# One unbroken line of expert tiles, independent scatters, and ranks by prefix sums, in a fused attention and mixture-of-experts kernel

## The chip, the core and the metric

The kernel runs on one core of a Trainium2 chip. The core has five engines, each with an instruction queue of its own that it works off in order: PE (TensorE, matmul and transpose), DVE (VectorE), ACT (ScalarE), POOL (GpSimd) and SP (SyncE, which issues most of the DMAs). Engines wait for each other, and for DMAs, by semaphores. PE loads the stationary operand of a matmul with a separate instruction, which the profile lists as PEld. The metric is the device time of one execution in microseconds; a profile adds, for one execution, a record of each instruction.

## The reference

Four batches of 1024 rows of 128 numbers pass through four residual stages, each on a normalised copy of the rows. In short form:

```
x = x + attention_a(layernorm(x))   # 8 heads of 128, with a relative-position term
x = x + experts(layernorm(x))       # 8 experts, the best 2 for each row
x = x + attention_b(layernorm(x))   # causal, 16 query heads of 8, one key/value head
x = x + experts(layernorm(x))       # the same weights again

def experts(x):
    scores = softmax(x @ Wg.T)                    # 8 per row
    val, idx = top_k(scores, 2)
    val = val / (val.sum(-1) + 1e-9)
    comb = (one_hot(idx) * val[..., None]).sum(-2)
    out = 0
    for e in range(8):
        a, b = split(x @ W1[e].T + b1[e], 2)      # 256 each
        out += ((a * sigmoid(b)) @ Wo.T + bo) * comb[..., e]
    return out
```

Everything is in float32.

## The kernel before

**Stages.** The program is attention a, experts f, attention b, experts g, in this order; f and g are the two uses of the experts. All of x stays in SBUF. In each stage the order of instructions on every engine is that in which the program's text issues them: the order is written by hand, as Python generators that are advanced in turn, one `yield` being one place where something else may be put between. An engine that meets an instruction whose input isn't there stands still, and so does all that is queued behind it.

**The experts' method.** A row is computed for its two experts only. The 2048 (row, expert) pairs of a batch are sorted by expert, each expert's share is rounded up to whole tiles of 128 rows, and so a batch never needs more than `TILES` = 23 tiles, of which each belongs to one expert. The sorted rows lie in DRAM (`sorted_rows[b]`), and so do the experts' results (`stores`).

**`dispatch` (L203 to L343)** sorts one batch for one of the two stages:

- `norm_steps` (L87): means and variances on DVE, `rstd` as a power on POOL (L101), `shift` on DVE (L103), eight scalings on ACT. Then POOL sets the last column of the copy to 1 (the row sums to zero, so that column is known from the rest, and the experts' weights are prepared so that it carries the bias).
- Two halves of four transposes each, `lnps` (L217), copied to SBUF by ACT; eight small matmuls for the gate, `gp` (L223); softmax and the two best experts on DVE (L247 to L281), with a mask of 128 x 8 tiles x 8 experts for each choice.
- `rank`: how many earlier pairs go to the same expert. `sel` is the sum of the two masks. One matmul with `before` (a strict triangle of ones) counts the earlier rows within a tile (L287), and eight with `ones`, each 8 columns narrower than the last, add the tiles before (L289). A ninth tile of zeros at the end makes the totals.
- From these on DVE the place of each pair (`places`), and the expert of each of the 23 tiles (`experts`, L322 to L330).
- Sixteen scatters (L335), indirect DMAs issued by POOL, each of which writes 128 rows into `sorted_rows[b]`. The framework sees sixteen writes to one tensor.

The parameters `far` and `at_once` say how many yields separate the dispatch's parts, and after how many scatters one comes. The first three dispatches of f run inside attention a, one beside each of its later batches (from L676); the fourth runs beside the first steps of experts f. Those of g run beside attention b once a batch's rows are finished (in `causal_attention`, L1051), and what is left by its end runs in experts g.

**`experts_tiles` (L728)** computes one batch as twelve pairs of tiles with two further steps to drain. A step p does, in this order: a `fetch` (L710) of four tiles of sorted rows from DRAM into one of four slots of `ring`, issued by SP; `first`, one matmul of 512 columns for each of two tiles (`h`, L745), a sigmoid on ACT (L749) and a product on DVE (`u`, L751); `turn_hidden` of the pair before, four transposes (L759) and a copy on ACT (L767); in every second step `turn_rows`, four transposes of the next fetched tiles (L733, the tile is named `xgps`) with a copy on ACT (L735); and `second` of the pair two back (`yp`, L777), whose bias is added on DVE (L784) before SP stores the result (L788). The two drain steps hold no `first`. The next batch's first two fetches are issued in them, and its first `turn_rows` follows at once.

**`combine` (L812)** brings a batch's results back: sixteen gathers by indirect DMA on POOL (L833), and for each the weighted addition to x on DVE (L820). `at_once` sets how many gathers go out in a step, and an addition is issued once 2 * `at_once` further gathers have been. For g the finished rows then leave for the output.

**`ffn` (L850)** runs the batches one after the other, and advances beside each step the generators listed for it: the fourth dispatch, the combines, and two calls of `b_prep` (L878, the queries and keys of attention b for batches 0 and 1). Seen as one list, f has 56 steps:

```
0: [sends("f", B - 1, (2, 2))], 20: [combine("f", 0, 1)], 37: [combine("f", 1, 2)], 39: [b_prep(0)],
48: [combine("f", 2, 2)], 49: [b_prep(1)],
```

In g the dispatches that are left are chained: one ends before the next begins. The last combine of g stands behind all of it, and nothing runs beside it.

Of the kernel before, what the change touches and what calls it, by code (L numbers as in the profile page):

```python
# [18 lines left out]
P = 128  # L19
# [45 lines left out]
def block_kernel(ctx: ExitStack, tc: tile.TileContext, a: dict, out: bass.AP):  # L65
# [21 lines left out]
    def norm_steps(x_b, name, got, xn=None, fine=False):  # L87
# [13 lines left out]
        nc.gpsimd.tensor_tensor(rstd, ve, nhalf, ALU.pow)  # L101
        shift = work.tile([P, NB], F32, tag="ln_sh", name=f"sh_{name}")
# [4 lines left out]
        for t in range(NB):  # L107
            nc.scalar.activation(
                xn[:, t, :], x_b[:, t, :], AF.Identity, bias=shift[:, t : t + 1],
                scale=rstd[:, t : t + 1],  # L110
            )
            if t == 3 or (t % 2 and fine):
                yield
# [44 lines left out]

    earlier = wp.tile([P, E, E], F32, tag="earlier", name="earlier")
# [41 lines left out]
    chosen, sent_off = {}, set()  # L201

    def dispatch(which, b, bank, new_xn, new_xnT, far, at_once):  # L203
# [15 lines left out]
        for _ in range(far):  # L219
            yield  # L220
# [35 lines left out]
        sel = part(NB + 1)  # L256
        dv.memset(sel[:, NB, :], 0.0)
# [16 lines left out]
        dv.tensor_tensor(sel[:, :NB, :], masks[0], masks[1], ALU.add)  # L274
# [11 lines left out]
        flat = sel.rearrange("p t e -> p (t e)")  # L286
        nc.tensor.matmul(rank[:, : (NB + 1) * E], before, flat, start=True, stop=False)  # L287
        for k in range(1, NB + 1):
            nc.tensor.matmul(  # L289
                rank[:, k * E : (NB + 1) * E], ones, flat[:, : (NB + 1 - k) * E],  # L290
                start=False, stop=(k == NB),
            )
# [28 lines left out]
        began = part(TILES)[:1]  # L321
# [10 lines left out]
        yield  # L332
        for t in range(NB):
            for k in range(2):
                nc.gpsimd.indirect_dma_start(  # L335
# [3 lines left out]
                )  # L339
                if t == NB - 1 and k == 1:  # L340
                    sent_off.add((which, b))
# [9 lines left out]
    with ExitStack() as sa:  # L351
# [278 lines left out]
        with tc.manual_schedule():  # L630
            for t in range(-AHEAD, N + 5):
# [44 lines left out]
                if m >= H and m % H < H - 3:  # L676
                    if m % H == 0 and i == 0:
# [4 lines left out]
                            2, 1,  # L682
# [17 lines left out]
    def sends(which, b, pace=(2, 1)):  # L700
        return dispatch(
            which, b, one,
            lambda: fp.tile([P, NB, D], F32, tag="xn", name=f"xn_{which}{b}", bufs=1),
            lambda: fp.tile([P, L], F32, tag="xnT", name=f"xnT_{which}{b}", bufs=1),
# [3 lines left out]
    chunks = (TILES + 3) // 4  # L708
    pairs = (TILES + 1) // 2
    fetched = []  # L710

    def fetch(which, b, c):
        assert (which, b) in sent_off, (which, b)
        n = min(4, TILES - 4 * c)
        xg = ring[:, len(fetched) % 4]
        fetched.append((b, c))
        nc.sync.dma_start(
            out=xg[:, :n, :],
            in_=sorted_rows[b].rearrange("(t p) d -> p t d", p=P)[:, 4 * c : 4 * c + n, :],
        )  # L720
        return xg, n

    def experts_tiles(which, b, stored, come):


        nm = f"{which}{b}"
        experts = chosen[which, b][2]
        turned, hidden, outs = {}, {}, {}  # L728

        def turn_rows(c, xg, n):  # L730
            ps = one(f"xgps_{nm}_{c}")
            for t in range(n):
                nc.tensor.transpose(ps[:, t * P : (t + 1) * P], xg[:, t, :], ident)  # L733
            xgT = fp.tile([P, 4, P], F32, tag="xgT", name=f"xgT_{nm}_{c}", bufs=2)
            nc.scalar.copy(xgT[:, :n, :].rearrange("p t c -> p (t c)"), ps[:, : n * P])  # L735
            turned[c] = xgT

        def first(j):
            at = nc.values_load(
                experts[0:1, j : j + 1], engines=[mybir.EngineType.PE], min_val=0,  # L740
                max_val=(E - 1) * 512,
                skip_runtime_bounds_check_because="one less than a sum of E comparisons, times 512",
            )
            ps = one(f"h_{nm}_{j}")
            nc.tensor.matmul(  # L745
                ps, turned[j // 4][:, j % 4, :], w1[:, bass.ds(at, 512)], start=True, stop=True
            )
            sig = fp.tile([P, HID], F32, tag="sig", name=f"sig_{nm}_{j}", bufs=3)
            nc.scalar.activation(sig, ps[:, HID:], AF.Sigmoid)  # L749
            u = fp.tile([P, HID], F32, tag="u", name=f"u_{nm}_{j}", bufs=4)  # L750
            nc.vector.tensor_tensor(u, ps[:, :HID], sig, ALU.mult)  # L751
            hidden[j] = u

        def turn_hidden(p):
            js = [j for j in (2 * p, 2 * p + 1) if j < TILES]
            ps = one(f"turn_{nm}_{p}")
            for q, j in enumerate(js):
                for k in range(2):
                    nc.tensor.transpose(  # L759
                        ps[:, (2 * q + k) * P : (2 * q + k + 1) * P],  # L760
                        hidden[j][:, k * P : (k + 1) * P], ident,
                    )
                del hidden[j]
            uT = fp.tile([P, 4, P], F32, tag="uT", name=f"uT_{nm}_{p}", bufs=2)
            n = 2 * len(js) * P
            uf = uT.rearrange("p k c -> p (k c)")
            nc.scalar.copy(uf[:, :n], ps[:, :n])  # L767
            return uT, js

        def second(p, uT, js):  # L770
            if p % 2 == 0:
                outs[p // 2] = small(f"yp_{nm}_{p}")
            yp = outs[p // 2]
# [436 lines left out]
```

## Time and profile before

| what | us |
|---|---|
| median of 3 runs (lowest, highest) | 2942.23 (2940.53, 2950.89) |
| the profiled execution, its own time | 2939.64 |
| its span, first to last instruction | 2937.9 |
| mean granted PE clock | 0.952 of full |

| group, in experts g and around it (2654 to the end) | count | busy us | mean ns |
|---|---|---|---|
| h, PE, L745 | 184 | 99.5 | 669 |
| yp, PE, L777 | 368 | 50.8 | 283 |
| turn, PE, L759 | 184 | 29.2 | 280 |
| xgps, PE, L733 | 92 | 15.6 | 294 |
| scatters, POOL, L335 | 32 | 31.0 | 970 |
| gathers, POOL, L833 | 64 | 61.0 | 953 |
| u, DVE, L751 | 92 | 38.0 | 423 |
| uT copies, ACT, L767 | 48 | 27.2 | 568 |

How to read it: a group collects the instructions of one line. PE's float32 matmuls appear as two records each, and records overlap, so that sums of a group's busy time exceed the time it occupies; the distance between the starts of successive groups is what it takes. A row of the timeline gives start, duration, engine, line, operation, output and inputs, shape, count, and in brackets the time the engine had stood idle before it and what ended that. "issue" is a wait that the profile doesn't explain, "remote" a semaphore whose sender it doesn't name.

### The profile page before, as it was taken

What the parts mean: (1) busy time and instruction counts of PE and PEld (TensorE: products, weight loads), DVE (VectorE), ACT (ScalarE), POOL (GpSimd) and SP (SyncE); (2) the same over time, 40 slices, a digit from 0 to 9 for tenths busy, and PEclk for the clock granted to TensorE, in tenths of its full rate; (3) what the DMA queues carried; (4) which work ended last, traced back from release to release, by engine and by line L of the source; (5) the groups of instructions that cost most, each with busy time, mean ns of one, the idle gap of its engine ahead of it and who ended that gap; (6) DMA issues with size and microseconds to landing.
All of it is one profiled execution on the core that took longest, in us unless ns stands there. A gap on an engine that the chain in (4) does not pass through costs nothing. (4 is left out here: it accounts for less than half of the span.)

```text
span 2937.9 us, 46362 instructions
## 1 busy us (share of the span) xinstructions
PE 2768.5 (94%) x18784; PEld 1699.4 (58%) x18784; DVE 1393.6 (47%) x3012; ACT 1334.8 (45%) x2460; POOL 491.1 (17%) x453
## 2 busy tenths in 40 slices
PE   6999999999999999999999887999999999998765
PEld 3465666656665656565656655655465465554543
DVE  2345444454545454545453433556355455662323
ACT  2434344444445344434343343555555655554422
POOL 3121000002000011000010024432121231221154
PEclk9999999999999999999999999899889898999887
DMA  8577566656557565666565123100000000000233
GB/s 212 194 237 238 170 209 191 204 168 213 190 183 221 174 198 190 206 197 210 198 216 169 40 81 86 27 10 1 1 1 1 6 24 1 9 7 25 57 95 91
DMA packets 148485, 363.53 MB, mean 124 GB/s; under 512 B 16160, under 2 KB 71872, under 8 KB 147952
## 3 DMA queue, kind: packets, MB, share of 16 engines
q1 hardware_dynamic: 130128, 316.78, 33.5%
q0 software_dynamic: 15552, 40.97, 5.3%
q10 hardware_dynamic: 2592, 2.82, 0.4%
q8 instruction: 149, 2.44, 0.4%
q14 instruction: 64, 0.52, 0.1%
HBM read 176.69 MB, written 183.76 MB: 123 GB/s over the span
## 5 line engine op out<-in xcount | busy, mean ns | idle before, releaser
L555 DVE CUSTOM_DVE_ANT_0 s<-sp,s 128x1024 f32<-128x1024 f32 x256 | 313.1, 1223 | 392.5 <-PE sp L550 390.7
L550 PE MATMUL sp<-kT,xT 128*128 128x512 f32 x1024 | 484.7, 596 | 3.7 <-ACT kT L509 2.1
L560 ACT ACTIVATE s<-s,nmax 128x1024 f32<-128x1024 f32 x256 | 294.0, 1149 | 416.8 <-DVE nmax L555 416.8
L994 PE MATMUL t_b<-qm,ka_b 32*128 32x512 f32 x1152 | 459.3, 683 | 10.0 <-DVE m L949 8.0
L582 PE MATMUL op<-at,xrep 32*128 32x256 f32 x8192 | 453.0, 377 | 8.6 <-DVE rinv L572 8.6
L582 PEld LDWEIGHTS op<-at,xrep 32*128 32x128 f32 x8192 | 418.6, 186 | 54.5 <-issue 32.9
L942 PE MATMUL s_b<-ka_b,qa_b 32*128 32x128 f32 (+3 forms) x2304 | 439.6, 431 | 2.0 <-DVE xnT_g L248 1.6
L997 ACT ACTIVATE pt_b<-t_b 128x512 f32<-128x512 f32 x576 | 329.3, 611 | 206.3 <-PE t_b L994 163.9
L949 DVE TENSOR_REDUCE m<-s_b 128x1 f32<-128x512 f32 (+3 forms) x480 | 288.9, 650 | 142.9 <-PE s_b L942 119.7
L942 PEld LDWEIGHTS s_b<-ka_b,qa_b 32*128 32x128 f32 x2304 | 275.9, 204 | 74.1 <-issue 21.6
L569 DVE STREAM_TRANSPOSE at<-s 128x1024 f32<-128x1024 f32 x256 | 315.8, 1238 | 0.2 <-ACT s L560 0.2
L522 PE MATMUL rp<-relk,xT 128*128 128x512 f32 x640 | 303.4, 596 | 0.0
L527 ACT COPY xr<-rp 128x1024 f32<-128x1024 f32 x256 | 256.5, 1002 | 84.6 <-issue 52.9
L550 PEld LDWEIGHTS sp<-kT,xT 128*128 128x128 f32 x1024 | 175.0, 191 | 129.4 <-issue 123.3
L994 PEld LDWEIGHTS t_b<-qm,ka_b 32*128 32x128 f32 x1152 | 166.6, 197 | 93.4 <-DVE m L949 50.0
L592 DVE COPY oT<-op 128x256 f32<-128x256 f32 x64 | 24.2, 420 | 401.8 <-PE op L582 401.8
L522 PEld LDWEIGHTS rp<-relk,xT 128*128 128x128 f32 x640 | 116.9, 190 | 131.0 <-issue 129.3
L590 ACT COPY oT<-op 128x256 f32<-128x256 f32 x64 | 20.7, 375 | 355.9 <-PE op L582 355.9
L1015 PE MATMUL o_b<-pt_b,va_b 128*32 128x512 f32 x1152 | 159.6, 678 | 0.0
L335 POOL DMA_INDIRECT sorted<-xn_f,places_f x64 | 62.2, 972 | 466.2 <-DVE places_f L318 311.8
L522 PE MATMUL rp<-w,xT 128*128 128x512 f32 x256 | 121.1, 595 | 0.0
L745 PE MATMUL h_g<-w,xgT_g 128*128 x184 | 99.5, 669 | 14.4 <-ACT xgT_g L735 13.6
(264 smaller groups left out, 3006.1 us busy)
## 6 DMA issues: line engine op xcount, KB each, us to landing
skew<-xr SPq DMA_DIRECT2D x256, 576.0 KB
s<-skew SPq DMA_DIRECT2D x256, 512.0 KB
ring<-sorted SPq DMA_DIRECT2D x40, 256.0 KB
xrep<-stored POOLq DMA_DIRECT2D x16, 512.0 KB
sorted<-ident POOLq DMA_DIRECT2D x4, 1472.0 KB
res_f<-y_f SPq DMA_DIRECT2D x20, 256.0 KB
res_g<-y_g SPq DMA_DIRECT2D x20, 256.0 KB
w<-in_w POOLq DMA_DIRECT2D x16, 256.0 KB
```

What stands on the lines that cost most here:

```text
L522: nc.tensor.matmul(rp[:, c, :], lhsT, rk[:, base + c * 512 : base + (c + 1) * 512], start=True, stop=True)
L527: nc.scalar.copy(xr[:, :L], rp.rearrange("p a c -> p (a c)"))
L550: nc.tensor.matmul(sp[:, c, :], xTs[b][:, i * P : (i + 1) * P], kT[:, c * 512 : (c + 1) * 512], start=True, stop=True,)
L555: nc.vector.tensor_tensor_reduce(out=s, in0=sp.rearrange("p a c -> p (a c)"), in1=s, scale=-1.0, scalar=BIG, op0=ALU.add, op1=ALU.min, acc ...
L560: nc.scalar.activation(s, s, AF.Exp, bias=nmax, scale=-1.0, accum_out=total)
L569: nc.vector.transpose(sums[m][:, i, :], s)
L582: nc.tensor.matmul(ops[g // 2][:, g % 2, :256], xrep[r, j, :], at[r, :, j * 32 : (j + 1) * 32], start=(j == 0), stop=(j == 31),)
L942: nc.tensor.matmul(ps[:, q * w : (q + 1) * w], qa[rows[g], k + q, tok], ka[rows[g], k0 : k0 + w], start=True, stop=True,)
L949: nc.vector.tensor_reduce(m2[:, 4 * g + k : 4 * g + k + nh, c], ps[:, : nh * w].rearrange("p (k c) -> p k c", c=w), AX.X, ALU.max,)
L994: nc.tensor.matmul(ps, ka[rows[g], j * P : (j + 1) * P], qm[rows[g], :], start=True, stop=True)
L997: nc.scalar.activation(pt[:, g, :], ps, AF.Exp, scale=HD ** -0.5)
L1015: nc.tensor.matmul(op[g * 32 : (g + 1) * 32, :], va[:, j, :], pt[:, g, :], start=(j == i), stop=(i == 0 or j == i - 1),)
```

## The change

Four things are changed together.

**One line of experts.** `experts_tiles` no longer runs once a batch. It runs over all 48 steps of the four batches, with three more to drain. In step s: the fetch for step s + 4, then `first` of step s, `turn_hidden` of step s − 2 (s − 1 before), in even steps `turn_rows` for step s + 2, and `second` of step s − 3 (s − 2 before). The turned rows and the hidden values lie in two buffers with four slots each.

```diff
+        rows_T = hold[0].rearrange("p (s t) c -> p s t c", s=4)
+        hidden = hold[1].rearrange("p (s q k) c -> p s q k c", s=4, q=2)
...
+        n = len(steps_of)
+        for s in range(-4, n + 3):
+            if s % 2 == 0 and s // 2 + 2 < len(chunks):
+                fetch(s // 2 + 2)
+            if 0 <= s < n:
+                first(s)
+            if 0 <= s - 2 < n:
+                turn_hidden(s - 2)
+            if s % 2 == 0 and 0 <= s // 2 + 1 < len(chunks):
+                turn_rows(s // 2 + 1)
+            if 0 <= s - 3 < n:
+                second(s - 3)
+            if s >= 0:
+                yield
```

**Scatters.** The sixteen of a batch are declared independent of each other, a memset of one number on POOL stands before each, and each fetch of the batch is made to wait for all sixteen.

```diff
+                nc.gpsimd.memset(between, 0.0)
+                put = nc.gpsimd.indirect_dma_start(
                     out=sorted_rows[b],
...
+                if written_at[which, b]:
+                    tc.declare_no_dep(
+                        put.ins, group=nm, query=mybir.DependencyQuery.ANY_SYNC,
+                        reason="rows at other places",
+                    )
+                tc.add_to_no_dep_group(nm, put.ins)
+                written_at[which, b].append(put.ins)
```

**Ranks.** DVE sums the tiles before each tile by doubling (pairs, fours, eights), with three more additions and a larger memset. PE then does two matmuls of 72 columns, where it did nine.

```diff
-        dv.tensor_tensor(sel[:, :NB, :], masks[0], masks[1], ALU.add)
+        dv.tensor_tensor(sel[:, 1 : NB + 1, :], masks[0], masks[1], ALU.add)
+        dv.tensor_tensor(one_two[:, 2:, :], sel[:, 1 : NB + 1, :], sel[:, :NB, :], ALU.add)
+        dv.tensor_tensor(up_to_four[:, 4:, :], one_two[:, 2:, :], one_two[:, :NB, :], ALU.add)
+        dv.tensor_tensor(
+            sums_before[:, 1:, :], up_to_four[:, 4:, :], up_to_four[:, :NB, :], ALU.add
+        )
...
-        flat = sel.rearrange("p t e -> p (t e)")
-        nc.tensor.matmul(rank[:, : (NB + 1) * E], before, flat, start=True, stop=False)
-        for k in range(1, NB + 1):
+        for k, (w, v) in enumerate(((before, sel[:, 1:, :]), (ones, sums_before))):
             nc.tensor.matmul(
-                rank[:, k * E : (NB + 1) * E], ones, flat[:, : (NB + 1 - k) * E],
-                start=False, stop=(k == NB),
+                rank[:, : (NB + 1) * E], w, v.rearrange("p t e -> p (t e)"),
+                start=(k == 0), stop=(k == 1),
             )
```

**The order around them.** `norm_steps` yields between the power on POOL and `shift`; `dispatch` yields between the halves of `lnps`; scatters in attention a go out two a step. The normalised copies that `sends` uses have two buffers each (one before). `combine` sends two gathers a step and adds six gathers behind; the last one of g sends four a step and adds four behind. The dispatches left over for g run side by side, no longer chained. The lists are:

```diff
-            0: [sends("f", B - 1, (2, 2))], 20: [combine("f", 0, 1)], 37: [combine("f", 1, 2)], 39: [b_prep(0)],
-            48: [combine("f", 2, 2)], 49: [b_prep(1)],
+            0: [sends("f", B - 1, (1, 2))], 22: [combine("f", 0)], 33: [combine("f", 1)],
+            36: [b_prep(0)], 43: [combine("f", 2)], 46: [b_prep(1)],
...
-        rest = itertools.chain(*left, *(sends("g", b, (2, 2)) for b in unsent))
         left = ffn("g", {
-            0: [rest], 21: [combine("g", 0, 1)], 38: [combine("g", 1, 2)], 47: [combine("g", 2, 2)],
+            0: [*left, *(sends("g", b, (1, 2)) for b in unsent)], 22: [combine("g", 0)], 31: [combine("g", 1)], 41: [combine("g", 2)],
         })
```

As the program is built, POOL's queue in g then holds, in this order, `rstd` of batches 2 and 3, the sixteen scatters of batch 2 with the memset of batch 3's copy among them, those of batch 3, and the gathers; before, `rstd` of batch 3 stood behind all scatters of batch 2, and batch 3's scatters alternated with gathers. The second matmul set and the `rank` of batch 2 move into the first steps of experts g, and five of `b_prep(1)`'s fourteen steps stay in experts f, where seven of thirteen did; the rest moves into attention b.

## The prediction

> **What bounds the kernel now.** I read the page's busy shares, then the same shares by stage, then the idle gaps of PE in the two expert stages in the timeline. The stages are attention a (0 to 1650 us), experts f (to 1872), attention b (to 2654), experts g (to the end).
>
> ```profile
> PE 2768.5 (94%) x18784; PEld 1699.4 (58%) x18784; DVE 1393.6 (47%) x3012; ACT 1334.8 (45%) x2460; POOL 491.1 (17%) x453
> ```
> ```profile
> 0.00:1650.00 1650.00, 1602.29 (x11773) 999.53 (x11774) 770.02 (x1626) 700.56 (x1222) 136.40 (x159) 1.00 0.62 196
> 1650.00:1872.00 222.00, 193.09 (x1020) 132.44 (x1021) 87.09 (x258) 100.35 (x216) 77.12 (x76) 0.94 0.26 71
> 1872.00:2654.00 782.00, 770.38 (x4957) 435.17 (x4956) 444.74 (x852) 436.44 (x813) 183.71 (x121) 0.90 0.02 6
> 2654.00:2938.00 284.00, 202.75 (x1042) 132.27 (x1040) 91.73 (x277) 97.41 (x209) 93.84 (x99) 0.84 0.25 69
> ```
>
> Columns of the last four: stretch, its length, busy PE, PEld, DVE, ACT, POOL (instructions), PE's granted clock, DMA share, GB/s. PE is the bound of both attentions: it idles 48 us of 1650 and 12 of 782. In the expert stages it idles 29 of 222 and 81 of 284. What the change can win lies there and in PE work it strikes out.
>
> What an undisturbed expert step costs, from PE's timeline in f:
>
> ```profile
> 1661.85 1.88 PE L745 MATMUL h_f<-w,xgT_f 128*128 x4
> ...
> 1665.33 1.98 PE L745 MATMUL h_f<-w,xgT_f 128*128 x4
> ...
> 1668.48 1.88 PE L745 MATMUL h_f<-w,xgT_f 128*128 x4
> ```
>
> From the first h to the third, two steps (four tiles, one turn_rows) take 6.63 us. So 23 tiles take 38.1 us and four batches **152.5 us**. The stages take more: in f PE runs from 1650.94 to 1861.2 (210.3 us); in g from the first h at 2686.0 to the last yp at 2907.5 (221.5 us). The rest is gaps. Three kinds:
>
> ```profile
> 1743.40 0.63 PE L733 MATMUL xgps_f<-ident,ring 128*128 128x128 f32 x4 [3.15 <-DMA ring<-sorted]
> 1744.71 5.40 PE L745 MATMUL h_f<-w,xgT_f 128*128 x8 [0.67 <-ACT xgT_f L735]
> ```
> ```profile
> 2728.63 0.17 DVE L103 SCALAR_TENSOR_TENSOR sh_g<-mv_g,rstd_g 128x8 f32<-128x8 f32 x1 [18.07 <-POOL rstd_g L101]
> ```
> ```profile
> 2854.18 0.37 ACT L767 COPY uT_g<-turn_g 128x256 f32<-128x256 f32 x1 [9.30 <-remote]
> 2865.43 0.58 ACT L735 COPY xgT_g<-xgps_g 128x512 f32<-128x512 f32 x1 [10.88 <-remote]
> ```
>
> First, a batch boundary: the line drains, the next batch's rows arrive late, then PE's clock is granted at 0.50 for 3.4 us (stretch 1745.3 to 1748.7) and the first h come slowly: 5.40 us for 8 records that take about 3.7 in the steady rows. Second, DVE stands 18 us for a POOL instruction that is queued behind 16 scatters; PE gaps 13.72 us at 2729.3. Third, ACT takes PE's finished results 9 to 11 us late; PE gaps 8.51 and 9.25 us. The last falls in a train of 21 POOL gathers without a pause (2835.7 to 2861.8); a train of 18 in f (1767.9 to 1790.1) has the same in small, PE gaps 2.31, 2.37 and 2.72 us. The trace names no cause.
>
> **Scatters.** They run one at a time, gathers do not:
>
> ```profile
> 2713.42 0.96 POOL L335 DMA_INDIRECT sorted<-xn_g,places_g  x1 [1.54 <-DMA sorted<-xn_g,places_g]
> 2715.92 0.96 POOL L335 DMA_INDIRECT sorted<-xn_g,places_g  x1 [1.55 <-DMA sorted<-xn_g,places_g]
> ...
> 2913.42 0.94 POOL L833 DMA_INDIRECT got_g<-res_g,places_g  x1 [0.30 <-issue]
> 2914.67 0.94 POOL L833 DMA_INDIRECT got_g<-res_g,places_g  x1 [0.30 <-issue]
> ```
>
> Period 2.50 against 1.25 us. Freed, and with the tiny memset before each (an 8-wide one takes 0.11), I take 1.4 to 1.5 us: 16 in 23 us instead of 40. On POOL alone this buys nothing, since PE does not wait for POOL's length; it buys by what is queued behind. The new fetch waits for all 16 of its batch; g3's should end by about step 21 (one step is 3.3 us), and its first fetch is at step 32, so that wait has some 10 steps of cover. If they stayed serial it would still be met, but the g0 gathers behind them would come late (rival C).
>
> **Experts in one line.** Nothing but the batch borders is removed: same transposes, matmuls, copies. Fetch now stands 2 steps (6.6 us) ahead of turn_rows and turn_rows 2 steps ahead of h, where before a boundary started them all at once. Removed in f: boundary gaps 0.86+1.68+0.73, 3.15+0.67+0.73, 2.77+0.67+0.92 = 12.2 us, and the slow restarts, about 1.5 us each, 4.5. In g: 2.60+0.67+0.92 and 3.01+0.68+0.73 = 8.6, 3 for restarts, and the 9.25 gap, counted with the trains. Longer lags (turn_hidden 2, second 3 steps) add a fill and a drain of one step, hidden nowhere but once per stage: 1.5 us.
>
> f, built up: start 2.4 + steps 152.5 + dispatch f3 3.0 (lnps 0.87, gp 1.71, rank 0.43) + b_prep(0) 11.2 = 169, against 210.3: −41. Kept: 3 us of the train's 7.4, since f0's 16 gathers are still free. **f: −37** (0.9 us of lnps_b1 moves to attention b).
>
> g, built up: 152.5 + dispatches 3.5 (g3 3.0, rank_g2 0.43) + the first steps at a half clock, as now, 2.6 + drain 1.5 = 160, against 221.5: −61. The 13.7 us gap goes because rstd_g3 now stands ahead of g2's scatters on POOL, and shift is one yield later on DVE; what is late next is memset xn_g3, behind six of them (9 us), and PE needs that batch only at step 36. The rank_g2 wait (3.16 us, DVE chain) and its work leave the stretch before the first h: −4. Kept of the trains' 18.5: 8. **g: −57.** The tail after the last yp (store, 16 gathers at 1.25, adds, out: 30.4 us) holds the same instructions: 0.
>
> **Combines** start later for f0 (step 22 for 20) and with lag 6, so an add on DVE stands behind its gather less often; before, one waited 5.33 us at 1771.8 and PE gapped 4.40, in g 3.89. f's is inside the −41, g's inside the −61. The price, adds that crowd near attention b, is DVE time beside a busy PE: 0.
>
> **Ranks.** Eighteen records fall to four, eight times:
>
> ```profile
> 1714.54 0.34 PE L287 MATMUL rank_f<-xnT_f,before 128*128 128x72 f32 x2
> 1714.71 1.90 PE L289 MATMUL rank_f<-xnT_f,ones 128*128 128x64 f32 x16
> 1716.47 0.68 PE L745 MATMUL h_f<-w,xgT_f 128*128 x1
> ```
>
> From 1714.54 to 1716.47 is 1.93 us, 0.107 a record whether 72 or 8 columns wide. Four records: 0.43; saved 1.5, eight times **12 us**. The Trainium skill ("TensorE: Matmul & The Clock Gate", Back-to-back issue gap) gives the isolated gap as columns/2.4 + 2.5 ns, and warns that it under-counts small widths. By it the old 360 columns in 9 matmuls, as two records each, are 0.35 us, the new 144 are 0.13: saved 0.2, or 1.8 in all. The row decides: 12. Three more adds on DVE, 72 wide, are some 0.2 us each (estimated from the 0.17 of the 128x8 one above); they lie on the dispatch's own chain, which PE does not wait for in attention.
>
> **Attention a.** A block without dispatch takes 47.09 us; the three with one take 48.33, 52.55, 50.69: +10.3. PE work is 4.5 of it, gaps 0.98 (DVE waits for rstd), 1.74 (second lnps half waits for ACT), 0.69, 0.79. The two yields spread the first two: with ranks −4.2 a dispatch, 12.6 for three. New DVE adds and freed scatters can hurt here: bounds 0 to −12.6 (a loss is rival B), I take **−10**, near the gaps seen.
>
> **Attention b.** Ranks of g0 and g1 −3, b_prep(1)'s late half +2, forced in a burst: **−1**, ±4 as k3, k4 and vp have no row in that place.
>
> Sum: −10 −37 −1 −57 = **−105 us**. Against the profiled execution (2939.64; span 2937.9 plus 1.7 around it) 2834.6; the median of the runs shown is 2.6 higher and their spread 10. Forecast **2834**.
>
> **Rivals.** (B) *Long POOL trains decide.* Free scatters make six new trains of 16 (f0 to f2 in attention a, f3, g2, g3; those of g0 and g1 are broken by affine selects). If each holds back ACT and DVE like the two seen, it costs from 7.4 us (f's) to its whole length, 23, where PE meets it without buffers (g's cost 18.5), and the gather trains keep their full price (+15): 2834 + 15 + 44 to 138 = 2893 to 2987, middle 2940. It decides against the change from 15.2 us a train. For it: two trains of 18 and 21 show it from about the ninth DMA on. Against: each scatter has a memset before it and, past the eighth, a wait for an earlier one's landing; in attention there are more buffers between PE and ACT. Chance 0.15, half of it over 2940.
> (C) *The scatters stay serial* by some other wait. g0's gathers then start at step 29, its adds at 25: DVE waits, some 8 us: 2842. Against: the order of POOL shows no such wait. 0.08.
> (D) *All late starts go*, because lag 6 and the memsets take their cause away: −11 kept, −8 more in attention: 2815. 0.12.
> Main: 0.65.
>
> **How the numbers follow.** The main case runs 2816 to 2855: −12.6 to 0 in attention a, ±4 in b, trains free or at full price (−11 to +15). C and D are within. B is left out, and D's lower part; the ends go a little beyond the main case on both sides for sizes that I mistook: **2806 to 2875**. 0.5% is 14.7 us, about what a measurement here can tell. Below 2925 lie main, C, D and a third of B: 0.90; a third of B is within (0.05), a third slower (0.05).
>
> **What would show it.** Right: from the first h to the last yp 160 us in g, and 169 for PE in f; no ring wait over 1 us at a border; no DVE wait on rstd of 18 us; scatters 1.4 to 1.5 us apart; the three dispatch blocks together 145 to 147; the tail 30 us as before. Wrong: late ACT starts beside scatter trains, attention a longer than 1650, or DVE adds waiting on gathers in g.

## The result and the profile after

| | median us | runs | changed / before |
|---|---|---|---|
| the kernel before | 2947.40 (2937.23 to 2959.76) | 20 | |
| the changed kernel | 2960.31 (2945.73 to 2969.65) | 20 | 1.0038 [1.0021, 1.0054] |

The forecast was 105 us less; the change came out 13 us (0.4%) slower. The profiled execution took 2969.65 us, the slowest of its twenty; its span is 2967.9, the mean granted clock 0.945.

The page's busy shares, and the four stages (columns as before: stretch, length, busy PE, PEld, DVE, ACT, POOL, clock, DMA share, GB/s):

```profile
PE 2760.7 (93%) x18672; PEld 1691.6 (57%) x18672; DVE 1393.6 (47%) x3036; ACT 1333.0 (45%) x2462; POOL 499.6 (17%) x581
```
```profile
0.00:1674.60 1674.60, 1610.98 (x11740) 1003.79 (x11741) 772.75 (x1638) 700.64 (x1222) 140.30 (x207) 0.99 0.59 193
1674.60:1889.10 214.50, 176.89 (x903) 118.80 (x901) 80.96 (x251) 90.84 (x198) 68.77 (x86) 0.90 0.25 72
1889.10:2705.00 815.90, 800.52 (x5178) 453.18 (x5177) 448.82 (x873) 459.61 (x863) 194.81 (x159) 0.91 0.02 7
2705.00:2937.70 232.70, 172.21 (x856) 115.82 (x856) 82.66 (x252) 81.93 (x180) 80.62 (x114) 0.86 0.25 73
```

These borders follow PE's own marks: first xgps_f, last yp_f, first h_g, last yp_g. In the same measure the kernel before took 1651.1, 210.2, 824.8 and 221.6 us. The waits at the batch borders are gone and experts f and g still became longer, 214.5 and 232.7; attention a, too, lost 23 us. PE idles 38 us of experts f and 61 of g.

The DVE timeline in attention a, beside the second train of scatters (1091.9 to 1111.9), shows one such idle time; PE's and POOL's rows of the same time stand below it.

```profile
1103.12 1.23 DVE L574 CUSTOM_DVE_ANT_0 s<-sp,s 128x1024 f32<-128x1024 f32 x1 [2.15 <-PE sp L569]
...
1105.43 0.12 DVE L591 RECIPROCAL rinv<-total 128x1 f32<-128x1 f32 x1
1114.46 1.23 DVE L574 CUSTOM_DVE_ANT_0 s<-sp,s 128x1024 f32<-128x1024 f32 x1 [8.91 <-remote]
```
```profile
1104.66 1.02 PE L569 MATMUL sp<-kT,xT 128*128 128x512 f32 x2
1105.52 1.88 PE L541 MATMUL rp<-relk,xT 128*128 128x512 f32 x4
...
1115.75 1.22 PE L523 MATMUL kp<-xT,joint 128*128 128x512 f32 x1 [5.97 <-DVE nmax L574]
```
```profile
1108.43 0.96 POOL L347 DMA_INDIRECT sorted<-xn_f,places_f  x1 [0.22 <-issue]
1109.38 0.09 POOL L346 MEMSET between<- 1x1 f32 x1
1109.69 0.96 POOL L347 DMA_INDIRECT sorted<-xn_f,places_f  x1 [0.22 <-issue]
```

PE had finished this sp at 1105.68 (the end of PE's first row). DVE was free from 1105.55 and read it at 1114.46: 8.8 us late. Elsewhere it reads an sp 0.04 us after its end when it is free. PE soon runs out of work and waits for DVE (its last row). The scatters follow each other every 1.26 us; the memset fits into the 0.30 us that POOL left between gathers anyway. In experts g, beside a train of sixteen scatters and sixteen gathers (2779.2 to 2819.2), ACT and DVE stand for 18 and 20 us in front of finished results (DVE's row is followed by PE's row with the result that it reads, which ended at 2787.02, while DVE was free from 2788.64):

```profile
2813.16 0.38 ACT L775 ACTIVATE sig_g<-h_g 128x256 f32<-128x256 f32 x1 [18.36 <-remote]
```
```profile
2808.95 0.69 DVE L806 TENSOR_TENSOR y_g<-yp_g,fbo 128x512 f32<-128x512 f32 x1 [20.32 <-remote]
```
```profile
2785.96 1.06 PE L799 MATMUL yp_g<-fwo,uT_g 128*128 128x128 f32 x8
```

Another reading is possible: `s` and `y` are also moved by DMA, so DVE could be waiting for a transfer that the trains delay. The trace speaks against it. SP's transfers go through queue q1, and of the queues only these moved packets in the stretch from 2786 to 2808 (packets, MB, share):

```profile
q0 software_dynamic: 553, 1.12, 14.9%
q14 instruction: 1, 0.01, 0.1%
```

POOL's indirect DMAs are in q0; in q1 nothing was under way. In the first case the transfer that brings this `s` had been issued at 1084.95, 29.5 us before DVE began. ACT's copies of turned rows and hidden values, which read nothing but results of PE, are late in the same trains, by up to 9.4 us.

This is what rival B describes. Summed over all readings in the experts' line, the time in which PE's result and its reader were both ready and nothing began (where it is over 0.5 us) is 63 us in f and 117 in g, against 27 and 41 in the profile of before.

### The profile page after: what moved, and what is told of

It is laid out like the page before. It is cut to its first block, busy times and chain, and to the rows that moved or that the text cites. A ratio compares the mean times of both kernels' runs of the same rounds, so it can differ in the third digit from the quotient of the medians.

```text
span 2967.9 us, 46265 instructions
## 1 busy us (share of the span) xinstructions
PE 2760.7 (93%) x18672; PEld 1691.6 (57%) x18672; DVE 1393.6 (47%) x3036; ACT 1333.0 (45%) x2462; POOL 499.6 (17%) x581
## 5 line engine op out<-in xcount | busy, mean ns | idle before, releaser
L966 POOL TENSOR_SCALAR_AFFINE_SELECT dg<-dg 128x2048 f32<-128x2048 f32 x32 | 64.1, 2004 | 287.1 <-ACT dg L958 287.1
```

## The experiments

There were eighteen runs, on several chips, which the results number. That turned out to matter: the ratio is always to the kernel before, executed beside it on the same chip. "S" is the theory that indirect DMAs that follow each other too closely hold back the signals by which PE tells ACT and DVE that a result is there.

### Four kernels on chip 14: no train costs anything

**e1_serial** takes the independence away from the scatters.

```diff
-                if written_at[which, b]:
-                    tc.declare_no_dep(
-                        put.ins, group=nm, query=mybir.DependencyQuery.ANY_SYNC,
-                        reason="rows at other places",
-                    )
-                tc.add_to_no_dep_group(nm, put.ins)
```

> The changed kernel, its scatters dependent on each other again: each waits for the landing of the one before (2.50 us apart, as before the change). Theory S (indirect DMAs that follow each other every 1.25 us hold back the signals of PE, so that ACT and DVE begin late): the three attention blocks with scatters fall from 58.2, 60.5 and 60.4 us to 47 to 48.5 us, no reading of sp comes more than 3 us after PE ended it, PE's gaps of 10 to 15 us in experts f and g fall to those beside gather trains; in all 30 to 70 us less than the changed kernel, 2890 to 2930. Theory R (the sums on DVE and the moved yields cost the time): attention a stays at its length and the total stays within 10 us of the changed kernel's.

**e2_spaced**, **e3_sweep** and **e4_groups** keep it, and set POOL work between the scatters: a power on some columns of a tile that holds ones. e2 takes six columns; e3 takes 2, 3 and 4 in the dispatches f0, f1 and f2; e4 sends the scatters of these three in groups of four, eight and eight, with three, six and three pauses of eight columns before each group.

```diff
-                nc.gpsimd.memset(between, 0.0)
+                nc.gpsimd.tensor_tensor(between[:, :6], between[:, :6], nhalf[:, :6], ALU.pow)
```

> The changed kernel, its scatters independent, but with POOL work of some 1.3 us (a power on 6 columns) in place of the one-number memset before each, so that they stand about 2.5 us apart and wait for nothing. Theory S: as with serial scatters, attention blocks of 47 to 48.5 us and a total within 10 us of e1_serial. Theory W (what costs is that scatters overlap or are not waited for one by one, whatever their distance): as the changed kernel, within 10 us.

> As e2_spaced, but the three dispatches in attention a with pauses of 2, 3 and 4 columns of the power (estimated distances of 1.6, 1.9 and 2.1 us). Theory S with a limit of rate: the late readings of sp (8.8 us in the changed kernel) shrink from dispatch to dispatch and the blocks with scatters go from above 50 to 47 to 48.5 us. Theory L (what counts is the ninth indirect DMA in a row, at any rate below 2.5 us): all three blocks lose about 11 us as in the changed kernel.

> As e2_spaced, but the dispatches in attention a send their scatters back to back (1.25 us) in groups: fours with a pause of some 5 us before each, eights with some 10 us, eights with some 5 us. Theory L (it starts with about the ninth in a row, and a pause empties the backlog): no reading of sp over 3 us late with fours and with eights and 10 us, and at most a small loss with eights and 5 us. Theory S (any close following holds PE's signals): late readings in each group, and block lengths above 50 us in all three.

Measured: e1 2822.45 us, 0.966 [0.9637, 0.9682]; e2 2818.99, 0.9651 [0.9616, 0.9686]; e3 2808.64 and e4 2829.70 in one execution each; the kernel before 2922.60. All are 90 us or more faster than before, which looked like S confirmed. But e3 (distances 2.0, 2.15 and 2.3 us) and e4 (fours and eights at 1.26 us) show no late reading at all, in any variant, and in all four the trains of 29 to 33 indirect DMAs, nearly all gathers, leave PE gaps of no more than 6.2 us in sum, where the prediction counted 7.4 and 18.5 us for trains of 18 and 21 before the change. The kernel before itself was 25 us faster here. So what had changed could be the chip, and these four told nothing about S until the changed kernel ran beside them.

### The controls: the same kernel is fast on some chips and slow on others

> The changed kernel as it is, on the same chip as the next ones. The runs so far were on another chip than the comparison of the two kernels, whose kernel before was some 25 us slower there. Theory S (close trains of scatters hold back PE's signals): on any chip slower than e5_two_us by 100 us or more, near the time of before. Theory C (the chip, not the distance, made the first experiments fast): within 20 us of e5_two_us.

> The kernel before as it is, for its trace on this chip: in its trace of the comparison ACT and DVE began up to 9.5 us late beside the trains of 18 and 21 gathers (26.6 us of such waiting in experts f, 40.7 in g), while e1_serial and e3_sweep had trains of 29 and 33 gathers with hardly 7. Theory C' (the price of gather trains differs from chip to chip or run to run): here less than 15 us in each stage. Theory G (the two kernels' gathers differ in what they run beside): as before, 25 and 40.

> The changed kernel as it is once more, to see on which kind of chip this call runs. Theory M (in the comparison of the two kernels something of the machine, not of the kernel, let PE's signals through late beside trains of indirect DMAs): either 0.96 of the kernel before and no reading of sp over 2 us late, as in c_after, or 1.00 and readings 7 to 9 us late in each of the three trains, as in the comparison; nothing between.

> The changed kernel again, for its chip. Theory M: either about 0.96 of the kernel before, with sp read at once in the trains, or about 1.00 with readings 7 to 9 us late beside the trains.

> The changed kernel as it is, as a control for e10_breath_2 on the same chip. On a chip that holds PE's signals back: 1.00 of the kernel before, sp read 7 to 9 us late beside each train in attention a. On one that does not: 0.962.

| changed kernel, unedited | chip | median us | before there | ratio |
|---|---|---|---|---|
| the comparison | (not numbered) | 2960.31 | 2947.40 | 1.0038 [1.0021, 1.0054] |
| c_after | 14 | 2807.66 | 2919.89 | 0.9624 [0.9604, 0.9644] |
| c_after_2 | 10 | 2805.32 | 2920.22 | 0.9618 [0.9568, 0.9668] |
| c_after_3 | 15 | 2949.33 | 2946.61 | 1.0021 [1.0000, 1.0042] |
| c_after_4 | 9 | 2963.07 | 2947.09 | 1.0058 [1.0017, 1.0099] |

Theory M holds in these five: two kinds, nothing between. (Chip 14 served in two sets of runs, and was fast in both; each of the others in one set, so that there a property of the chip and one of the moment are not told apart.) The trace of c_after has the same trains at the same distance (a scatter train from 1083.5 to 1103.7), and DVE takes every sp at once:

```profile
1095.64 1.22 DVE L574 CUSTOM_DVE_ANT_0 s<-sp,s 128x1024 f32<-128x1024 f32 x1 [1.23 <-PE sp L569]
...
1099.30 1.23 DVE L574 CUSTOM_DVE_ANT_0 s<-sp,s 128x1024 f32<-128x1024 f32 x1 [1.22 <-PE sp L569]
```

PE ended these two at 1095.60 and 1099.26. On chip 9 (c_after_4) readings in the three scatter trains are up to 8.9 us late again, and the waiting in the experts sums to 62 us in f and 117 in g. On chip 14, c_before shows 4 us in f and 5 in g where the profile of before showed 27 and 41, beside a train of 37 indirect DMAs: theory C' holds. Its experts f and g are 11 and 15 us shorter there, which is most of the 27 us by which the kernel before is faster on this chip.

### Where trains cost, the distance decides

**e5_two_us** is e2 with the power on 2 columns (scatters 2.0 us apart). **e10_breath** adds four one-number memsets before each gather but those of the last batch (1.62 us apart at the least). **e11_limit** is e10 with three, five and eight such memsets in place of the power in the three dispatches of attention a. The cut shows e10's two edits, with the runs' helpers written out.

```diff
-                nc.gpsimd.memset(between, 0.0)
+                nc.gpsimd.tensor_tensor(between[:, :2], between[:, :2], nhalf[:, :2], ALU.pow)
                 put = nc.gpsimd.indirect_dma_start(
...
+            if (which, b) != ("g", B - 1):
+                for _ in range(4):
+                    nc.gpsimd.memset(between[:1, :1], 1.0)
             nc.gpsimd.indirect_dma_start(
                 out=rows_of[t][:, k, :], out_offset=None, in_=stores[which, b],
```

> The changed kernel with the shortest pause of e3_sweep before every scatter (a power on 2 columns, scatters 2.0 us apart in attention). Theory S: no late reading of sp, attention blocks of 48 to 49.5 us where scatters run, 2800 to 2825 on a chip whose kernel before takes 2922, 0.960 to 0.967 of it.

> The changed kernel with scatters about 2 us apart, beside c_after_3 on the same chip. If c_after_3 is disturbed: theory S says 60 us or more faster than it, no reading of sp over 2 us late, since its trains of scatters are gone; if the chip holds back PE's signals at any distance, as slow as c_after_3. If c_after_3 is not disturbed: equal to it within 10 us.

> The changed kernel with scatters 2.0 us apart and four one-number memsets on POOL before each gather but those of the last batch (estimated distance 1.6 us, so that two gathers still fit into an expert step of 3.3 us). On a chip like 15, theory S: the late readings beside gather trains shrink too, 20 us or more faster than e5_again (2863, 0.972 of the kernel before). On a chip like 14 or 10: 0.962 to 0.970. If gathers of 1.6 us are still too close: 0.972 on a chip like 15.

> Scatters 2.0 and gathers 1.6 us apart once more. Theory S: on either kind of chip 0.957 to 0.970 of the kernel before, with no reading of a PE result more than 2 us late; on a chip that holds signals back that is 80 us or more faster than c_after_4.

> As e10_breath, with the scatters of the three dispatches in attention a after three, five and eight memsets (estimated 1.5, 1.7 and 2.0 us apart). On a chip like 15 theory S with a limit between 1.26 and 2.0 us: the late readings of sp, 7 to 9 us in c_after_3, go down from dispatch to dispatch, and the block with the scatters from above 55 us to 49.5 to 51.2. On a chip like 14 or 10: blocks of 49.5 to 51.2 in all three.

| | chip | median us | ratio | changed kernel there |
|---|---|---|---|---|
| e5_two_us | 14 | 2812.92 | 0.9630 [0.9597, 0.9664] | 0.9624 |
| e5_again | 15 | 2862.57 | 0.9724 [0.9629, 0.9819] | 1.0021 |
| e10_breath | 13 | 2821.32 | 0.9576 [0.9552, 0.9601] | not run |
| e10_breath_2 | 9 | 2810.24 | 0.9540 [0.9501, 0.9579] | 1.0058 |

On chip 15 spacing the scatters alone brings 87 us, and its attention blocks with scatters go from 58.7, 58.5 and 58.6 us to 51.2, 51.2 and 49.5. What is left there lies in the experts, where the gathers still go out every 1.25 us (35 us of waiting in f, 57 in g). On chip 9 both spacings together bring 153 us. The stages of c_after_4, then those of e10_breath_2, on that same chip:

```profile
0.00:1669.80 1669.80, 1605.39 (x11740) 1000.31 (x11741) 772.95 (x1638) 700.62 (x1222) 140.62 (x207) 0.99 0.60 193
1669.80:1882.70 212.90, 175.63 (x903) 118.53 (x901) 81.01 (x251) 90.88 (x198) 68.93 (x86) 0.90 0.25 72
1882.70:2698.70 816.00, 798.93 (x5176) 451.94 (x5177) 451.89 (x873) 459.69 (x863) 195.07 (x158) 0.91 0.02 7
2698.70:2931.10 232.40, 172.38 (x856) 115.91 (x856) 82.97 (x252) 81.88 (x180) 80.58 (x114) 0.86 0.25 73
```
```profile
0.00:1644.90 1644.90, 1598.70 (x11741) 999.70 (x11742) 772.88 (x1638) 699.93 (x1222) 174.47 (x208) 1.00 0.61 196
1644.90:1816.40 171.50, 167.42 (x903) 114.64 (x901) 83.06 (x251) 92.37 (x198) 95.49 (x266) 0.99 0.31 90
1816.40:2604.60 788.20, 771.25 (x5177) 441.55 (x5177) 451.07 (x873) 458.62 (x863) 224.31 (x235) 0.94 0.02 7
2604.60:2774.70 170.10, 159.71 (x856) 109.30 (x856) 83.32 (x252) 83.56 (x180) 114.46 (x286) 0.97 0.34 98
```

POOL works 124 us more, PE's instructions are the same but for one, and attention a and experts f and g are shorter by 25, 41 and 62 us. In the experts of e10_breath_2 no reading waits 2 us, and the waiting sums to 1 us in f and 2 in g. DVE reads a yp beside the last scatter train of experts g, in c_after_4 20.35 us after it became idle, and in e10_breath_2 at once:

```profile
2802.74 0.69 DVE L806 TENSOR_TENSOR y_g<-yp_g,fbo 128x512 f32<-128x512 f32 x1 [20.35 <-remote]
```
```profile
2691.52 0.69 DVE L814 TENSOR_TENSOR y_g<-yp_g,fbo 128x512 f32<-128x512 f32 x1 [0.93 <-PE yp_g L807]
```

e10 is the version to use where trains cost: it beats both kernels on chip 9, and on chip 13 it is at 0.958. It did not run on chips 14 and 10; its experts g and its tail, 170 and 34 us, are some 6 and 4 us longer than those of c_after, so by an estimate from these it loses some 10 us there.

e11 shows no late reading at 1.5, 1.8 and 2.2 us (blocks 51.2, 51.2 and 49.5). The changed kernel did not run on chip 13, so it isn't shown that this chip holds signals back, but two signs say that it does. The kernel before takes 2941 us there, as on chips 15 and 9 (2947) and not as on 14 and 10 (2920). And its traces miss semaphore events, as all traces of chips 15 and 9 do: with scatters 2.0 us apart in attention a there are some 12 a microsecond on chips 13, 15 and 9, and 17 on chip 14. If so, 1.5 us is enough for scatters. Shown on chips 15 and 9 is that it begins between 1.26 us and 2.0 for scatters, and between 1.25 and 1.62 for gathers.

**e7_all_spaced** spaces more than is needed: scatters 2.5 and gathers 2.3 us.

```diff
-                nc.gpsimd.memset(between, 0.0)
+                nc.gpsimd.tensor_tensor(between[:, :5], between[:, :5], nhalf[:, :5], ALU.pow)
...
+            if (which, b) != ("g", B - 1):
+                nc.gpsimd.tensor_tensor(between[:, :4], between[:, :4], nhalf[:, :4], ALU.pow)
             nc.gpsimd.indirect_dma_start(
                 out=rows_of[t][:, k, :], out_offset=None, in_=stores[which, b],
```

> The changed kernel with a pause of POOL before every scatter (a power on 5 columns, about 2.5 us apart) and every gather but those of the last batch (4 columns, about 2.3 us). Where trains hold PE's signals back: 100 us or more faster than the changed kernel. Where they don't: 5 to 20 us slower, since gathers end later and additions on DVE wait for them.

On chip 10, where trains cost nothing: 2878.59 us, 0.9873 [0.9828, 0.9918], 73 us slower than c_after_2, which is far more than expected. A combine asks for two gathers a step; a step is 3.3 us and two gathers now 4.6, so DVE's additions wait for them. DVE's waits of this kind in experts f (us in sum, times, the longest), of which c_after_2 has none in that stage:

```profile
DVE x L843 <- DMA got_f<-res_f,places_f: 27.5, 15, 3.9
```

The readers of h, queued behind these additions, are held up with them: experts f take 194.4 us and g 199.4, which are 23 and 35 more than in c_after_2. The tail is 8 us longer, and attention b 18, where the clock differs too.

### The parts of the change, where trains cost nothing

**e6_ranks_back** is e5_two_us with the nine matmuls.

```diff
-        for k, (w, v) in enumerate(((before, sel[:, 1:, :]), (ones, sums_before))):
-            nc.tensor.matmul(
-                rank[:, : (NB + 1) * E], w, v.rearrange("p t e -> p (t e)"),
-                start=(k == 0), stop=(k == 1),
-            )
+        nc.tensor.matmul(rank[:, : (NB + 1) * E], before, flat, start=True, stop=False)
+        for k in range(1, NB + 1):
+            nc.tensor.matmul(
+                rank[:, k * E : (NB + 1) * E], ones, flat[:, : (NB + 1 - k) * E],
+                start=False, stop=(k == NB),
+            )
```

> As e5_two_us, with the ranks on PE again (nine matmuls, no sums on DVE). By the 0.107 us of each of the 14 records taken away (1.5 us for each of eight dispatches): 12 us slower than e5_two_us. By the count of columns: 2 us slower. If the longer chain on DVE costs more than PE saves: faster.

2811.21 us, 0.9624 [0.9608, 0.9640], against 2812.92 and 0.9630 [0.9597, 0.9664]: no difference of the whole that these runs can tell, though 12 us is at the edge of what they exclude. PE's rows at batch 3 of g, in e5 and then in e6:

```profile
2662.43 0.41 PE L302 MATMUL rank_g<-xnT_g,before 128*128 128x72 f32 x2 [1.94 <-DVE xnT_g L284]
2663.12 0.44 PE L302 MATMUL rank_g<-xnT_g,ones 128*128 128x72 f32 x2 [0.27 <-DVE xnT_g L287]
2663.61 3.20 PE L774 MATMUL h_g<-w,hold_g 128*128 x4
```
```profile
2666.62 0.41 PE L298 MATMUL rank_g<-xnT_g,before 128*128 128x72 f32 x2 [1.74 <-DVE xnT_g L287]
2666.87 1.90 PE L300 MATMUL rank_g<-xnT_g,ones 128*128 128x64 f32 x16
2668.62 1.96 PE L772 MATMUL h_g<-w,hold_g 128*128 x4
```

From the start of the first record to that of the next h: 1.18 us with the sums, 2.00 with nine matmuls. That is 0.8 us, of the 1.5 forecast. Of the rest, 0.27 us is a wait for DVE's longer chain between the two matmuls; the wait before them is 0.2 us longer as well (1.94 against 1.74). In this place the h after it comes slower (3.20 us against 1.96 for four records), because PE is granted half its clock from 2664.2 for 3.4 us in e5 and not in e6; that gives it all back. By stage e6 is the longer one in attention a, f and g, by 2.7, 2.3 and 1.4 us, of which 3.4 us more of half clock in each of the first two can be up to 1.7; it is 3.1 us shorter in attention b, where its half-clock time is 99 us against 113. So outside attention b the sums seem to save 3 to 6 us over six dispatches, by one trace of each, and the clock hides it in the whole.

**e8_old_yields** undoes the three moved yields. **e9_line_only** undoes the whole dispatch (serial scatters, ranks on PE, old yields) and keeps the one line.

```diff
         nc.gpsimd.tensor_tensor(rstd, ve, nhalf, ALU.pow)
-        yield
...
-            if t == 3 or fine:
+            if t == 3 or (t % 2 and fine):
...
-            yield
-        for _ in range(far - 1):
+        for _ in range(far):
             yield
```

> The changed kernel without the three moved yields of the dispatch (between the power and shift, after every scaled tile, between the halves of lnps). By the prediction's gaps in attention a (0.98 and 1.74 us in each of three dispatches): 8 us slower than the changed kernel there, attention a 8 us longer. Theory Y (the yields also made the clock of attention b better, whose half-clock time fell from 188 to 113 us): attention b 30 us longer too.

> The changed kernel with the dispatch of before: scatters serial, ranks on PE, yields as they were; what stays is the one line of experts with the lists and combines. If the line carries the gain: 0.965 to 0.975 of the kernel before (2820 to 2845 where it takes 2920), experts f and g each within 180 to 190 us. If the parts only work together: above 0.985.

e8: 2839.16 us, 0.9741 [0.9713, 0.9769], 34 us slower than c_after_2 on the same chip. Attention a takes 1651.1 us, 6.8 more, near the 8 expected; attention b is 39 us longer, as theory Y has it. Attention b in e8, then in c_after_2:

```profile
1820.20:2643.70 823.50, 804.68 (x5181) 458.45 (x5180) 463.02 (x914) 460.07 (x863) 197.91 (x162) 0.90 0.02 7
```
```profile
1815.80:2600.00 784.20, 770.69 (x5177) 441.40 (x5176) 447.95 (x873) 458.52 (x863) 194.88 (x159) 0.94 0.02 7
```

PE's instructions are the same within four, the clock 0.90 against 0.94. These are one trace each, but all four executions of e8 were granted a mean clock of 0.960 to 0.962, and the six of c_after and c_after_2 0.967 to 0.975.

e9: 2866.39 us, 0.9817 [0.9786, 0.9848], between its two expectations; f 170.4 us, g 181.2, of which one PE gap of 16.95 us is DVE behind rstd, queued behind serial scatters:

```profile
2686.39 0.17 DVE L103 SCALAR_TENSOR_TENSOR sh_g<-mv_g,rstd_g 128x8 f32<-128x8 f32 x1 [22.17 <-POOL rstd_g L101]
```

So on these chips the line with its lists gives about half of the gain (54 of 115 us), the yields some 34 us, mostly by the clock of attention b, and the freed scatters 15 us (e1 against c_after, partly the clock).

## Why the prediction was wrong

**The step that failed** is the price of the scatter trains. The prediction kept 3 us in f and 8 in g for gather trains, priced the six new scatter trains at nothing ("On POOL alone this buys nothing", "it buys by what is queued behind"), and put their cost in rival B at a chance of 0.15. Where the comparison ran, they decide. What close trains cost is measured on chip 9, where c_after_4 and e10_breath_2 differ in nothing but the pauses: 25 us in attention a, 41 in f and 62 in g, 153 in the median of the whole. The two trains that the prediction had seen showed a growing lateness from about the ninth DMA, and the change made six new ones, at 1.26 us where the scatters had been 2.5 us apart. That should have weighed more than the absence of a named cause. Two of the signs that the prediction had named for being wrong are in the profile: late starts beside scatter trains, and attention a at 1674.6 us, longer than 1650.

B's range, 2893 to 2987, holds the 2960 that was measured. By B's sum that is (2960 − 2834 − 15) / 6 = 18.5 us a train, just what the prediction had counted for the one in g; but this agreement is partly luck. In attention a the three trains cost 7, 11 and 9 us (the blocks below). In f and g, close trains cost 41 and 62 us, where one and two scatter trains of 18.5 us and 15 us for all gathers make 70.5 together. And attention b, 28 us longer in c_after_4 than in e10_breath_2 by its clock, is in none of these sums; whether the trains have a part in that is not shown.

**The arguments against B** did not hold. The memset was to stretch the distance to 1.4 to 1.5 us: measured 1.26. A wait for an earlier scatter's landing was to slow the second half: the sixteen run evenly. Attention's buffers were to cover the lateness: its three blocks with scatters took 58.2, 60.5 and 60.4 us, against 51.2, 49.5 and 51.2 in c_after.

**The sums for an undisturbed chip** can be checked on chip 14. The stages of c_before, then of c_after:

```profile
0.00:1649.40 1649.40, 1603.01 (x11783) 1000.92 (x11784) 770.60 (x1629) 700.89 (x1222) 136.47 (x159) 1.00 0.62 196
1649.40:1848.70 199.30, 179.59 (x922) 120.60 (x921) 82.10 (x252) 96.56 (x207) 67.48 (x69) 0.96 0.28 77
1848.70:2681.00 832.30, 812.80 (x5219) 461.38 (x5217) 455.71 (x896) 456.97 (x855) 193.63 (x127) 0.89 0.02 7
2681.00:2887.20 206.20, 173.18 (x866) 116.48 (x866) 74.69 (x213) 81.76 (x177) 79.06 (x82) 0.90 0.30 83
```
```profile
0.00:1645.40 1645.40, 1599.61 (x11741) 1000.01 (x11742) 773.29 (x1638) 699.96 (x1222) 140.47 (x207) 0.99 0.60 196
1645.40:1816.80 171.40, 167.37 (x903) 114.21 (x900) 81.33 (x251) 92.25 (x198) 68.77 (x86) 0.99 0.32 90
1816.80:2611.20 794.40, 780.96 (x5177) 445.91 (x5176) 447.79 (x873) 459.01 (x863) 194.91 (x159) 0.93 0.02 7
2611.20:2775.30 164.10, 157.08 (x856) 108.57 (x856) 83.63 (x252) 83.48 (x180) 80.70 (x114) 0.98 0.36 104
```

- *Experts in one line.* Built up without trains, the forecast was 169 us for f and 160 for g (the rest of its −57 for g lies ahead of the first h); measured 171.4 and 164.1. PE idles 4 and 7 us in them. No transpose of fetched rows waits for its fetch; where the trace tells the landing, it comes 2.6 to 4.9 us after issue, against 6.6 us of lead. The gain, 28 and 42 us, is smaller than the 41 and 61 forecast without trains, mostly because the kernel before is 11 and 15 us faster on this chip. That it came to a similar total, −112 us against −105, is partly luck, as the next points show.
- *rstd behind the scatters.* Right: in experts g of c_after shift follows with no wait on rstd (the row below); in e9, with the old order, DVE's wait of 22.17 us and PE's gap of 16.95 are back.

```profile
2630.57 0.16 DVE L104 SCALAR_TENSOR_TENSOR sh_g<-mv_g,rstd_g 128x8 f32<-128x8 f32 x1
```

- *Attention a.* −4 us for a forecast of −10. The first two blocks of a dispatch are shorter, as the yields were to make them (48.33 and 52.55 became 47.09 and 48.14), but the two blocks after grew from 50.69 and 47.09 to 51.27 and 49.5 to 51.2: part of the work moved one block on. Half-clock time in the stage rose from 10 to 17 us.
- *Ranks.* Forecast 12 us by the row, 2 by the page's formula. Taken in place, PE saves 0.8 us at batch 3 of g, where the row gave 1.5 and the formula 0.2; by stage e6 suggests 3 to 6 us over six dispatches, and in the whole nothing is seen. What was missed is that, in the experts, PE comes to rank before DVE has the sums.
- *Attention b.* Forecast −1, measured −38, of which the clock is some 35 (half-clock time 183 and 113 us; half of the difference). The prediction did not treat the clock at all outside the experts. Without this luck the total would be about −77 us where −105 was forecast.
- *Scatters.* Their distance was over-estimated (1.26, not 1.4 to 1.5). *The tail* is 30.2 us for 30.4, as forecast.
- *The range* reached 2875 and left all of B out. A lateness without a cause was treated as a remainder to be halved, when it was the largest uncertain term.

## What to carry to other kernels

Where a profile shows waits that no cause explains, count how many more of the same occasions a change makes, and price them in full. Take the kernel itself along as a control whenever experiments run elsewhere than the comparison did: four kernels here seemed to confirm a theory that their chip could not test. And indirect DMAs that are free of each other are better sent with a little distance (here 2.0 us for scatters and 1.6 for gathers) than back to back. The distance must not be longer than what consumes them allows: at 2.3 us for gathers e7 lost most of the gain.

## What the runs showed of the hardware that was not expected

**Signals of PE can be late while DMAs run close together.** On chips 15 and 9 and in the comparison, results that PE had finished were read up to 9 us late beside sixteen scatters 1.26 us apart in attention a, and up to 20 us after both were ready beside 32 indirect DMAs; on chips 14 and 10 nothing was late, with the same instructions. Signals between the other engines pass at once in the same stretches: SP issues its DMA 0.02 us after ACT's copy, and PE starts 0.06 us after the DVE row at 1114.46 ends.

The traces also differ in what they hold. In the train near 1100, c_after has 20 semaphore events a microsecond, c_after_4 and the comparison's about 5, so most events of that time are missing there. Late signals and missing events go together in these trains, which would fit a limit on how fast such events are passed on or recorded; but with scatters 2.0 us apart, events are missing on chips 15 and 9 too (some 12 for 17) while no sp is read late. Every run of this case lists a granted clock and so was recorded. Whether an unrecorded execution is held back as well was not tried, and the cause stays open.

**Attention b's length is its clock.** PE is granted half its clock there in stretches of 3.4 to 44 us, most of them in the middle of busy PE. Here is the first in c_after_2: two windows before it, then the stretch itself (length, then the busy time of PE, PEld, DVE, ACT and POOL, PE's granted clock, DMA share, GB/s):

```profile
1810.60:1814.00 3.40, 3.40 (x22) 2.39 (x21) 2.03 (x12) 1.66 (x4) 1.03 (x1) 1.00 0.26 77
1814.00:1817.40 3.40, 3.40 (x36) 3.28 (x36) 2.00 (x7) 0.83 (x3) 2.61 (x3) 1.00 0.07 19
1817.40:1834.40 17.00, 17.00 (x138) 16.86 (x137) 9.99 (x14) 8.73 (x19) 9.46 (x7) 0.50 0.12 32
```

In all twenty traces attention b takes from 784 to 834 us, and that length less half of the time at half clock is always 733 to 744: 784.2 less half of 88.7 is 739.8 in c_after_2, and 823.5 less half of 171.4 is 737.8 in e8, without the three yields. The Trainium skill ("TensorE: Matmul & The Clock Gate", What's actually happening) ties the half clock to idle windows of about 3.4 us. Here five of the eight stretches in c_after_2 come after 3.4 us in which PE's rows leave no idle time, which that rule does not explain. Why the yields matter is not settled: the clock also moves by itself, since e10, the same kernel, took 815 us there on chip 13 and 788 on chip 9, in one trace each.
